# An attention over adjacency lists: when the first q rows, the fifth overlapped list tile, the first gathers and the later lists take their places

## The chip, the core and the metric

The kernel runs on one core of a Trainium2 chip. The time is the device time in microseconds, the median of several runs. A profile of one more execution shows what each engine did: PE (TensorE: matmuls; its weight loads are PEld), DVE (VectorE), ACT (ScalarE), POOL (GpSimd) and SP (SyncE, which here only issues DMAs). Each engine works through its own stream of instructions in order; ACT and POOL also issue DMAs from their streams.

## The reference

One layer of a graph network on N = 4096 nodes with D = 512 features and 8 heads of 64. `adj` is a 4096 x 4096 mask, symmetric, with ones on its diagonal and about 17 ones in a row.

```python
hs, ht = layer_norm(x), layer_norm(h_target)         # ln1, both masked by nodemask
q = (ht @ Wq + bq).reshape(T, 8, 64) / 8
k = (hs @ Wk + bk).reshape(S, 8, 64)
v = (hs @ Wv + bv).reshape(S, 8, 64)
logits = where(adj != 0, q . k, -1e30)               # per head
attn = softmax(logits) @ v @ Wo + bo
ht = layer_norm(ht + attn)                           # ln2
out = layernorm(x + ht + gelu(ht @ W1) @ W2)
```

Since a row of `adj` has so few ones, the kernel computes the attention on lists of neighbours and not on the full matrix. A flag is raised when the lists don't hold for the input; then a general path over the full matrix would run. It does not run here.

## The kernel before

**Lists.** Rows of `adj` come in 32 tiles of 128, each tile in 4 quarters of 1024 columns (512 KB); the quarters are numbered q = 4 x tile + h. `quarter` (L708) issues a quarter's load on SP (L713). `edges` (L716) works on it: ACT turns it to bytes and counts (L728, Sign), DVE multiplies by positions (L733) and takes the 8 largest in each of 5 segments (L735); after the fourth quarter DVE decodes the candidates into a record of up to 24 neighbours (L742 to L759), and the undecoded rest is written out later (`keep_rest`, L766, on SP). Three byte buffers (`signs`) stand between ACT and DVE. `sort` (L807) ranks 16 tiles' rows by degree, and POOL scatters their records to memory in that order (L853), once for tiles 0 to 15 (part 0, NA = 16) and once for tiles 16 to 31 (part 1).

**One ring for everything.** `ring` (L566) is 20 slots of one k|v row (1024 floats) per partition. While the lists are made, slots 0 to 7 take adjacency quarters (DEEP = 8), slots 8 to 11 h_target rows and later the k|v rows on their way out, slots 12 to 16 rows of x (`xrows`, L578); slots 17 and 18 are the two `wide` buffers, slot 19 holds small tools. Quarters of the tiles below NA + FILL = 21 go through slots 0 to 7, later ones (q84 on) through the two `wide` buffers in turn (L709 to L712). In the attention the slots take gathered k|v rows, 17 of them in the first half and 20 in the second. `place` (L1025) fixes ahead of time which slots each slot group of up to S = 3 neighbours uses, round and round, from slot 0.

**Projections.** `project` (L864) goes through x in 16 groups of two row tiles. `source` (L919) computes k and v of one row tile: 4 matmul steps with Wk and 4 with Wv (L929; the profile shows 8 matmuls for each), ACT copies each half out of PSUM (L931), and one DMA on ACT's queue writes the row tile to `kvd` in memory (L935). Three PSUM buffers (`pq`) lie between PE and ACT.

**Fronts.** `front(i)` (L982) makes the q rows of sorted tile i: POOL gathers the h_target rows by record (L988), DVE writes the scales with a tie to what `latest` names (L994; the tie is a real operand, so the instruction can't come before that tile is written), ACT scales (L998), PE transposes (L1002), ACT applies ln1 (L1005), PE multiplies with Wq (L1011), DVE finishes (L1016). `first_fronts` (L1154) makes two of them ahead of the attention: both records are loaded (`prefetch`, L970, L979), and then both fronts are begun. `latest` is set by `source` from group 14 on (L932), to a column of k; once the attention runs it is set by each slot group.

**Attention.** For each slot group POOL gathers k|v rows by record (L966 through `issue`, L1058, up to 4 groups ahead, 5 in the second half), DVE multiplies k by q (L1220) and sums per head (L1225), ACT takes the exp (L1229, L1238) and scales one of three v rows (L1204), DVE scales the other two (L1184), and PE adds them up by transposing into PSUM (L1192). `finish` (L1077) normalises a tile (L1082 to L1103: DVE, ACT, PE in turn) and applies Wo (L1111, L1115) and ln2. `feed` (L1310) is the feed-forward network of a group of two tiles: PE L1325, gelu on ACT L1328, PE L1334, and `end` for the last layer norm.

**What sets the order.** Generators yield costs, and `_weave` (L400) always goes on with the stream that is least far; the scheduler below it then takes each engine's instructions in that order of priority, but lets a later one go first where an earlier one isn't ready by its own reckoning. What comes out is one fixed order per engine. Streams up to the attention: projections, `prepare` (lists 0 to 15, first sort, first fronts), `fill` (FILL = 5 more tiles of lists, 16 to 20). Streams from the attention on: attention, feed-forward, the other lists (`other_lists`, L1443, which begins at WAIT = 40 and takes 1.5 times each step's cost) followed by the second sort, and the loads of the last weights (L586, L587). UNIT = 60 is the cost of a group of two tiles.

Of the kernel before, what the change touches and what calls it, by code (L numbers as in the profile page):

```python
# [399 lines left out]
def _weave(*streams):  # L400

    live = [[t, n, g] for n, (g, t) in enumerate(streams)]
    asleep = []
    while live:
        s = min(live)
        cost = next(s[2], StopIteration)
        if cost is None:
            assert len(live) > 1  # L410
            asleep.append(s)
            live.remove(s)
            continue
        if cost is StopIteration:
            live.remove(s)
        else:
            s[0] += cost
        for w in asleep:
            w[0] = max(w[0], s[0])
        live += asleep  # L420
        asleep = []


def _take(gen, n):

    for _ in range(n):
        cost = next(gen, StopIteration)
        if cost is StopIteration:
            return
        yield cost  # L430
# [13 lines left out]
def adj_resnorm_kernel(  # L444
# [34 lines left out]
    N, D = x.shape  # L479
# [3 lines left out]
    NT = N // P  # L483
    G = 2
# [3 lines left out]
    NQ = 4  # L488
# [12 lines left out]
    NA, NBT = len(CAPS_A), len(CAPS_B)  # L501
# [31 lines left out]
    with tc.tile_pool(name="keep", bufs=1) as keep:  # L533
# [17 lines left out]
        with ExitStack() as late:  # L551
# [22 lines left out]
            def turn_of(name, places):  # L574
                turns[name] += 1
                return places[turns[name] % len(places)]
# [127 lines left out]
            adjs = []  # L704
            DEEP = 8
            FILL = 5

            def quarter(i, h):  # L708
                if i < NA + FILL:  # L709
                    a = ring[:, (i * NQ + h) % DEEP, :].bitcast(I32)  # L710
                else:
                    a = turn_of("wide", wide)  # L712
                nc.sync.dma_start(a, adj[i * P:(i + 1) * P, h * QW:(h + 1) * QW])  # L713
                return a

            def edges(i):  # L716

                part = 1 if i >= NA else 0
                rec = Rs[part][:, i - PARTS[part][0], :]
                cand = lp.tile([P, SEG, 8], U16, name="cand", bufs=2)  # L720
                for h in range(NQ):
                    n = i * NQ + h
                    while len(adjs) < min(n + 2, NT * NQ):
                        adjs.append(quarter(*divmod(len(adjs), NQ)))
                    a, adjs[n] = adjs[n], None

                    sg = turn_of("signs", signs)
                    nc.scalar.activation(sg, a, AF.Sign, accum_out=dpart[:, i, h:h + 1])  # L728
                    ahead = min(n + DEEP - 1, n + 3 + n // 2)
                    while len(adjs) < min(max(n + 3, min(ahead, (NA + FILL) * NQ)), NT * NQ):  # L730
                        adjs.append(quarter(*divmod(len(adjs), NQ)))
                    wd = sg.bitcast(U16)
                    nc.vector.tensor_tensor(wd, wd, lio, ALU.mult)  # L733
                    for s, (w0, w1) in enumerate(SEGS):
                        nc.vector.max(cand[:, h * SQ + s, :], wd[:, w0:w1])  # L735
                    if h == 1:
                        keep_rest()
                    if h % 2 and moms:
                        moments(moms.pop(0))
                    yield 2.0  # L740
                dec = dec_w
                nc.vector.tensor_single_scalar(dec[:, 0], cand, 255, op=ALU.bitwise_and)  # L742
                nc.vector.tensor_single_scalar(dec[:, 1], cand, 8, op=ALU.logical_shift_right)
                gid = lp.tile([P, 2 * SEG, 8], F32, name="gid")
                dec = dec.rearrange("p b s e -> p (b s) e")
                off = segoff.rearrange("p b q s -> p (b q s)")
                nc.vector.scalar_tensor_tensor(gid, dec, 0.0,
                                               off.unsqueeze(2).to_broadcast([P, 2 * SEG, 8]),
                                               op0=ALU.is_gt, op1=ALU.mult)
                nc.vector.tensor_add(gid, gid, dec)  # L750
                flat = gid.rearrange("p s e -> p (s e)")
                for r in range(RE // 8):
                    top = rec[:, E0 + r * 8:E0 + (r + 1) * 8]
                    nc.vector.max(top, flat)
                    if r + 1 < RE // 8:
                        nc.vector.match_replace(flat, top, flat, 0.0)
                held.append((rest_d[i * P:(i + 1) * P, :], flat))
                has = lp.tile([P, MAXE], F32, name="ehas")
                nc.vector.tensor_scalar(has[:, :RE], rec[:, E0:E0 + RE], 0.0, 0.0, op0=ALU.is_gt,  # L759
                                        op1=ALU.add, accum_out=cnt[:, i:i + 1])  # L760
                yield 4.0

            def keep_rest():

                while held:
                    nc.sync.dma_start(*held.pop())  # L766
# [33 lines left out]
            def moments(i):  # L800

                while asked and len(asked) > NT - 4 - i:
                    ask(asked.pop(0))
                t = hrow(i)
                stats(ip, t, mvh[:, i, :], "n0")
# [58 lines left out]
            def project(order, t=None):  # L864
# [54 lines left out]
                def source(n, j):  # L919
                    g, hT = order[n], state[n][1]  # L920
                    if asked or moms:
                        kvr = sp.tile([P, 2 * D], F32, name="tq", bufs=3)
                    else:

                        kvr = ring[:, 8 + (n * G + j) % 3, :]
                    for half, w in enumerate((wk, wv)):
                        pkv = psi.tile([P, D], F32, name="pq", bufs=3)
                        for kc in range(KC):
                            nc.tensor.matmul(pkv, hT[:, kc, j * P:(j + 1) * P], w[:, kc, :],  # L929
                                             start=kc == 0, stop=kc == KC - 1)  # L930
                        nc.scalar.copy(kvr[:, half * D:(half + 1) * D], pkv)  # L931
                    if n >= 14:  # L932
                        latest[:] = [kvr[:, 0:1]]
                    r0 = 1 + (g * G + j) * P
                    newest[:] = [nc.scalar.dma_start(kvd[r0:r0 + P, :], kvr).ins]  # L935
                    return 7.8
# [13 lines left out]
                for n in range(len(order)):  # L950
                    for j in range(G):
                        cost = source(n, j)
# [10 lines left out]
            recs, tqs, h2Ts, done, ready, latest, newest = {}, {}, {}, set(), [], [], []  # L963
# [6 lines left out]
            def prefetch(i):  # L970
                if i >= NT or i in recs:
                    return
                r0 = TILES[i][0]
                part = 1 if r0 >= PARTS[1][0] * P else 0
                assert part in done
                r0 -= PARTS[part][0] * P
                rec = sp.tile([P, E0 + MAXE], I32, name="rec", bufs=6)

                nc.gpsimd.dma_start(rec[:, :RW], recs_d[part][r0:r0 + P, :])  # L979
                recs[i] = rec  # L980
# [39 lines left out]
            EARLY = 2  # L1020
# [1 line left out]
            SG = [(i, j0, min(S, cap - j0)) for i, (_, cap) in enumerate(TILES)  # L1022
                  for j0 in range(0, cap, S)]
            kvs, rests, fronts = {}, {}, {}
            place = [0]  # L1025
            for i, _, n in SG:
                if place[-1] + n > RING[i >= NA]:
                    place[-1] = 0
# [6 lines left out]
            def step(gens, i):  # L1035

                if i in gens and next(gens[i], StopIteration) is StopIteration:
                    del gens[i]
# [111 lines left out]
            def go_on():  # L1150
                for i in list(fronts):
                    step(fronts, i)

            def first_fronts():  # L1154

                for i in range(EARLY):
                    prefetch(i)
                for i in range(EARLY):
                    fronts[i] = front(i)
                    step(fronts, i)  # L1160
                while not latest:
                    yield None
                while fronts:
                    go_on()
                    yield 4.0
# [210 lines left out]
            def chain(gens):  # L1376
                for g in gens:
                    yield from g

            WAIT = 40.0  # L1380
            AHEAD = 4
            UNIT = 60.0

# [36 lines left out]
            def fill():  # L1420
# [3 lines left out]
                yield 9.0  # L1424
                for cost in _take(ed, FILL * steps):
                    yield cost
# [16 lines left out]

            def other_lists():
                for cost in ed:
                    yield 1.5 * cost
                keep_rest()
                yield from sort(1)

            _weave((att, 0), (chain(feed(g) for g in range(len(GROUPS))), 0), (other_lists(), WAIT),  # L1450
                   (weights(), 0))

# [34 lines left out]
```

## Time and profile before

| | us |
|---|---|
| median of 3 runs (1814.98 to 1824.70) | 1821.21 |
| the profiled execution's own time | 1811.19 |
| its span | 1809.4 |
| busy in the span: PE / DVE / ACT / POOL | 1681.5 / 1435.1 / 1221.1 / 979.8 |
| PE busy from 290 to 350, of 60 us | 18.65 |
| median from issue to landing: an adjacency quarter / a k|v gather / a kvd write from the ring | 7.1 / 5.9 / 5.2 |

The profile's part 2 cuts the span in 40 slices of 45.2 us and shows for each the busy tenths of every engine, the granted clock of PE and the share and rate of the DMA engines. A line of the timeline has the start, the length, the engine, the line of the code, the operation with its output and input, how often, and in brackets how long the engine sat idle before it and what ended that. Tiles are named by the pool's tile: `kv` is the whole ring, so an adjacency quarter and a gathered k|v row both appear as `kv`. PE's clock is in shares of full speed, PE's ends are modelled, and the releaser in the brackets is inferred. An engine's queue of DMA issues has a q at its end (SPq, ACTq).

### The profile page before, as it was taken

The numbers are of one execution on the slowest core, as the hardware profiler recorded it, in microseconds if no ns is written. First come the engines' busy times: TensorE is split into PE (matmuls) and PEld (weight loads), VectorE is DVE, ScalarE is ACT, GpSimd is POOL, SyncE is SP. The second block draws the span as 40 slices with busy tenths as digits, with TensorE's granted clock in tenths as the row PEclk, the third lists the DMA queues.
The fourth block names the chain that finished last, engine by engine and source line by source line (L and its number), as shares of the span: only waits on it lengthen the run. The fifth ranks groups of instructions, "written<-read, shape, count | busy, mean of one in ns | idle before, by whom it ended". The sixth has DMA issues, their size and how long they took to land. (4 is left out here: it accounts for less than half of the span.)

```text
span 1809.4 us, 22969 instructions
## 1 busy us (share of the span) xinstructions
PE 1681.5 (93%) x7030; PEld 1101.4 (61%) x7030; DVE 1435.1 (79%) x2660; ACT 1221.1 (67%) x3119; POOL 979.8 (54%) x834
## 2 busy tenths in 40 slices
PE   7989984587999989999999989999999999999997
PEld 3434432465766666676776757666666666666664
DVE  6989886899999837777879989979879797988200
ACT  5767654486997636767768867877777676787211
POOL 1000144666566576667767788877575665663101
PEclk9999996698999999999999999999999999999998
DMA  9999968988887647778879888787776777774000
GB/s 343 370 376 375 344 228 293 405 276 321 294 300 237 230 159 258 240 253 279 281 256 320 288 263 292 252 281 261 242 273 216 255 239 247 247 246 149 18 6 26
DMA packets 140268, 463.26 MB, mean 256 GB/s; under 512 B 16500, under 2 KB 21672, under 8 KB 140136
## 3 DMA queue, kind: packets, MB, share of 16 engines
q0 software_dynamic: 96656, 342.64, 55.9%
q1 hardware_dynamic: 35664, 95.98, 15.0%
q10 hardware_dynamic: 7816, 23.08, 3.3%
q8 instruction: 58, 0.95, 0.2%
q14 instruction: 74, 0.61, 0.1%
HBM read 430.75 MB, written 30.89 MB: 255 GB/s over the span
## 5 line engine op out<-in xcount | busy, mean ns | idle before, releaser
L966 POOL DMA_INDIRECT kv<-kvd,rec x603 | 761.1, 1262 | 366.9 <-PE cps L1192 147.8
L1334 PE MATMUL po<-w,gt 128*128 128x512 f32 x1024 | 466.9, 598 | 10.3 <-ACT gt L1328 10.3
L1325 PE MATMUL pf<-h2T,w 128*128 128x256 f32 (+1 forms) x2176 | 466.5, 368 | 0.0
L1325 PEld LDWEIGHTS pf<-h2T,w 128*128 128x128 f32 x2176 | 389.7, 191 | 64.4 <-issue 19.8
L1220 DVE TENSOR_TENSOR kv<-kv,tq 128x1536 f32<-128x1536 f32 (+2 forms) x211 | 352.0, 1677 | 62.0 <-DMA kv<-kvd,rec 57.9
L1204 ACT ACTIVATE kv<-kv,pa 128x64 f32<-128x64 f32 x1520 | 390.9, 337 | 4.5
L1225 DVE TENSOR_REDUCE lg<-kv 128x24 f32<-128x1536 f32 (+2 forms) x211 | 350.4, 1668 | 1.2
L1334 PEld LDWEIGHTS po<-w,gt 128*128 128x128 f32 x1024 | 189.1, 192 | 207.2 <-issue 195.3
L1192 PE MATMUL cps<-ident,kv 128*128 128x128 f32 x2008 | 267.8, 282 | 47.7 <-DVE kv L1184 40.0
L1192 PEld LDWEIGHTS cps<-ident,kv 128*128 128x128 f32 x2008 | 242.2, 146 | 114.0 <-DVE kv L1184 45.8
L1184 DVE TENSOR_TENSOR kv<-kv,p 128x1024 f32<-128x1024 f32 (+1 forms) x211 | 251.3, 1195 | 23.8 <-ACT p L1229 22.5
L687 POOL TENSOR_TENSOR n_rs<-n_ve,mhalf 128x2 f32<-128x2 f32 (+2 forms) x51 | 48.6, 953 | 326.0 <-DVE n_ve L680 173.0
L728 ACT ACTIVATE kv<-kv 128x1024 uint8<-128x1024 int32 x128 | 134.9, 1055 | 94.5 <-DMA kv<-in_adj_dram 42.9
L1328 ACT ACTIVATE gt<-pf 128x512 f32<-128x512 f32 x128 | 76.3, 597 | 87.4 <-PE pf L1325 84.0
L1328 ACT ACT_TABLE_LOAD x103 | 132.1, 1283 | 1.7
L735 DVE MAX8 cand<-kv 128x8 uint16<-128x103 uint16 (+1 forms) x640 | 132.4, 253 | 0.5
L929 PE MATMUL pq<-wk,h2T 128*128 128x512 f32 x256 | 121.3, 619 | 8.3 <-ACT tq L931 5.7
L1229 ACT ACTIVATE p<-lg 128x24 f32<-128x24 f32 (+2 forms) x179 | 39.1, 218 | 120.5 <-DVE lg L1225 119.7
L1011 PE MATMUL t<-wq,tq 128*128 128x512 f32 x256 | 115.7, 595 | 2.1 <-ACT tq L1005 2.1
L929 PE MATMUL pq<-wv,h2T 128*128 128x512 f32 x256 | 115.4, 593 | 1.8 <-DVE rbc L662 1.0
L1115 PE MATMUL t<-wo,rb 128*128 128x512 f32 x256 | 115.2, 592 | 0.0
L929 PEld LDWEIGHTS pq<-wk,h2T 128*128 128x128 f32 x256 | 49.4, 199 | 65.3 <-issue 50.5
(160 smaller groups left out, 1581.8 us busy)
## 6 DMA issues: line engine op xcount, KB each, us to landing
kv<-in_adj_dram SPq DMA_DIRECT2D x128, 512.0 KB, 7.1
kvd<-tq ACTq DMA_DIRECT2D x24, 512.0 KB, 6.6
kv<-kvd,rec POOLq DMA_INDIRECT x603, 5.9
kv<-in_L_gnn_h_target_dram SPq DMA_DIRECT2D x32, 256.0 KB, 8.0
kv<-in_x_dram SPq DMA_DIRECT2D x15, 512.0 KB, 9.3
rest_d<-gid SPq DMA_DIRECT2D x32, 160.0 KB, 4.7
w<-in_L_gnn_W_dram SPq DMA_DIRECT2D x4, 1024.0 KB, 9.9
kvd<-kv ACTq DMA_DIRECT2D x8, 512.0 KB, 5.2
```

What stands on the lines that cost most here:

```text
L728: nc.scalar.activation(sg, a, AF.Sign, accum_out=dpart[:, i, h:h + 1])
L735: nc.vector.max(cand[:, h * SQ + s, :], wd[:, w0:w1])
L929: nc.tensor.matmul(pkv, hT[:, kc, j * P:(j + 1) * P], w[:, kc, :], start=kc == 0, stop=kc == KC - 1)
L966: nc.gpsimd.indirect_dma_start(out=dst, out_offset=None, in_=table[:, :], in_offset=bass.IndirectOffsetOnAxis(ap=idx, axis=0))
L1184: nc.vector.tensor_tensor(v4, v4, p[:, j0:j0 + m, :].unsqueeze(3) .to_broadcast([P, m, H, HD]), ALU.mult)
L1192: nc.tensor.matmul(cps[:, c, :], kv[:, j, D + c * P:D + (c + 1) * P], ident, is_transpose=True, start=j0 + j == 0 and c == 0, stop=j0 + n ...
L1204: newest[:] = [nc.scalar.mul(v, v, pa[:, hd:hd + 1]).ins]
L1220: nc.vector.tensor_tensor(kv[:, :n, :D], kv[:, :n, :D], tq[:, :D].unsqueeze(1).to_broadcast([P, n, D]), ALU.mult)
L1225: nc.vector.tensor_reduce(lg[:, :n, :], kv[:, :n, :D].rearrange("p j (h d) -> p j h d", h=H), AX.X, ALU.add)
L1325: nc.tensor.matmul(pf[:, k, :], w1[(f0 + k) // KC][:, kc, (f0 + k) % KC * P:((f0 + k) % KC + 1) * P], h2T[:, kc, :w], start=kc == 0, stop= ...
L1328: nc.scalar.activation(gt, pf, AF.Gelu_apprx_tanh)
L1334: nc.tensor.matmul(po[j], gt[:, k, j * P:(j + 1) * P], w2[(f0 + k) // KC][:, (f0 + k) % KC, :], start=False, stop=f0 + k == FC - 1, skip_g ...
```

## The change

Five edits. The tie of the first fronts names the last written half (v) of the last row tile instead of any k half from group 14 on. `first_fronts` loads a record and begins its front, tile by tile, instead of loading both records first. Tiles 0 to 19 use the ring's slots for their quarters (RINGED = 20), tile 20 uses the `wide` buffers. Slot groups are placed from slot 11 on. The other lists begin at 80 instead of 40 in the weave's cost and take 1.8 times each step's cost instead of 1.5. No engine gets other operations; the orders differ.

```diff
--- before.py
+++ after.py
@@ -704,9 +704,10 @@
             adjs = []
             DEEP = 8
             FILL = 5
+            RINGED = NA + FILL - 1
 
             def quarter(i, h):
-                if i < NA + FILL:
+                if i < RINGED:
                     a = ring[:, (i * NQ + h) % DEEP, :].bitcast(I32)
                 else:
                     a = turn_of("wide", wide)
@@ -727,7 +728,7 @@
                     sg = turn_of("signs", signs)
                     nc.scalar.activation(sg, a, AF.Sign, accum_out=dpart[:, i, h:h + 1])
                     ahead = min(n + DEEP - 1, n + 3 + n // 2)
-                    while len(adjs) < min(max(n + 3, min(ahead, (NA + FILL) * NQ)), NT * NQ):
+                    while len(adjs) < min(max(n + 3, min(ahead, RINGED * NQ)), NT * NQ):
                         adjs.append(quarter(*divmod(len(adjs), NQ)))
                     wd = sg.bitcast(U16)
                     nc.vector.tensor_tensor(wd, wd, lio, ALU.mult)
@@ -929,8 +930,8 @@
                             nc.tensor.matmul(pkv, hT[:, kc, j * P:(j + 1) * P], w[:, kc, :],
                                              start=kc == 0, stop=kc == KC - 1)
                         nc.scalar.copy(kvr[:, half * D:(half + 1) * D], pkv)
-                    if n >= 14:
-                        latest[:] = [kvr[:, 0:1]]
+                    if n * G + j == NT - 1:
+                        latest[:] = [kvr[:, D:D + 1]]
                     r0 = 1 + (g * G + j) * P
                     newest[:] = [nc.scalar.dma_start(kvd[r0:r0 + P, :], kvr).ins]
                     return 7.8
@@ -1022,7 +1023,7 @@
             SG = [(i, j0, min(S, cap - j0)) for i, (_, cap) in enumerate(TILES)
                   for j0 in range(0, cap, S)]
             kvs, rests, fronts = {}, {}, {}
-            place = [0]
+            place = [11]
             for i, _, n in SG:
                 if place[-1] + n > RING[i >= NA]:
                     place[-1] = 0
@@ -1155,7 +1156,6 @@
 
                 for i in range(EARLY):
                     prefetch(i)
-                for i in range(EARLY):
                     fronts[i] = front(i)
                     step(fronts, i)
                 while not latest:
@@ -1377,7 +1377,7 @@
                 for g in gens:
                     yield from g
 
-            WAIT = 40.0
+            WAIT = 80.0
             AHEAD = 4
             UNIT = 60.0
 
@@ -1443,7 +1443,7 @@
 
             def other_lists():
                 for cost in ed:
-                    yield 1.5 * cost
+                    yield 1.8 * cost
                 keep_rest()
                 yield from sort(1)
 
```

The new numbers of lines are one higher between `RINGED` and `first_fronts`, and the same after it.

## The prediction

> **What bounds the kernel now.** I read the page's parts 1 and 2 first, then a table of windows, then the timeline of the valley that part 2 shows, then ACT's waits.
>
> ```profile
> span 1809.4 us, 22969 instructions
> PE 1681.5 (93%) x7030; PEld 1101.4 (61%) x7030; DVE 1435.1 (79%) x2660; ACT 1221.1 (67%) x3119; POOL 979.8 (54%) x834
> PE   7989984587999989999999989999999999999997
> PEclk9999996698999999999999999999999999999998
> ```
>
> PE is busy to the end, while DVE, ACT and POOL run out some 100 us earlier. PE's instructions stay the same, so the time can only change by PE's idle time (1809.4 - 1681.5 = 127.9 us) and by the clock. Slices 6 and 7 (271 to 362 us) are the valley: there the projections end and the attention begins. The windows, in the order PE, PEld, DVE, ACT, POOL, clock, DMA share, GB/s:
>
> ```profile
> 290.00:310.00 20.00, 2.75 (x7) 0.95 (x5) 13.07 (x46) 5.75 (x10) 10.14 (x11) 0.67 0.90 316
> 310.00:330.00 20.00, 9.14 (x36) 7.06 (x36) 15.89 (x17) 8.49 (x33) 13.22 (x11) 0.50 1.03 407
> ...
> 430.00:450.00 20.00, 12.36 (x55) 10.40 (x56) 20.00 (x39) 14.88 (x47) 12.77 (x12) 0.66 0.89 338
> 450.00:500.00 50.00, 50.00 (x227) 35.20 (x226) 46.13 (x109) 45.63 (x110) 27.64 (x23) 1.00 0.85 288
> ```
>
> From 290 to 370 PE idles 17.3 + 10.9 + 13.2 + 4.4 = 45.8 us, from 410 to 450 another 1.5 + 7.6 = 9.1; from 450 on it is full, DVE or no DVE. The valley's timeline says why (start, length):
>
> ```profile
> 273.06 0.81 ACT L998 ACTIVATE tq<-tq,rec 128x512 f32<-128x512 f32 x1 [9.30 <-DVE gid L750]
> ...
> 282.38 1.06 ACT L728 ACTIVATE kv<-kv 128x1024 uint8<-128x1024 int32 x1 [4.05 <-DMA kv<-in_adj_dram]
> ...
> 290.03 0.33 ACTq L935 DMA_DIRECT2D kvd<-kv  x1
> ...
> 296.81 0.96 POOL L966 DMA_INDIRECT kv<-kvd,rec  x1 [20.42 <-ACT kv L728]
> ...
> 308.02 1.77 DVE L1220 TENSOR_TENSOR kv<-kv,tq 128x1536 f32<-128x1536 f32 x1 [1.98 <-DMA kv<-kvd,rec]
> ...
> 314.89 2.82 PE L1192 MATMUL cps<-ident,kv 128*128 128x128 f32 x12 [22.14 <-DVE kv L1184]
> ```
>
> L998, the scaling of the first q rows, holds ACT for 9.3 us while copies of k|v wait behind it. The last write of kvd goes out at 290.03; writes of kvd land after 4.3 to 6.0 us there, so at about 296; the first gather starts at 296.81. Its wait is put down to ACT's L728, but its slots 0 to 2 held adjacency quarters (q = 4 x tile + h) 80 to 82, which ACT read at 245.5 to 248.7. I take the landing of the last kvd write for the true releaser. ACT's waits from 220 to 460:
>
> ```profile
> ACT kv L728 <- DMA kv<-in_adj_dram: 22.3, 7, 4.1
> ```
>
> Those seven waits are of the tiles behind the ring (q84 on), which have two buffers only. They stand in ACT's order among the last copies of k|v.
>
> **What the Trainium skill says.** (1) "TensorE: Matmul & The Clock Gate", Architectural detail: ACT and DVE are strict FIFOs. The trace agrees: behind the 9.30 us of L998 no copy of k|v starts. (2) The same page, What's actually happening: after about 3.4 us without work the array runs at half clock. The clock of 0.50 at 310 to 330 agrees. (3) "DMA: Bandwidth & Descriptors", Anatomy of one DMA: about 2.0 us plus bytes/436e3; for a quarter of 512 KB that is an estimate of 3.2 us. The trace has 6.3 us from issue to landing at 245 to 262, 4.6 at 260 to 296 and 7.2 at 294 to 316; the measurements decide. (4) The same page, Issuing engines are not separate DMA queues: SP's loads and POOL's gathers share the DMA engines; 4.6 growing to 7.2 as the gathers begin agrees.
>
> **The change part by part**, against the profiled execution (1811.2 us with 1809.4 of span; the runs' median is 1821.2, 0.55% above it).
>
> *The tie moves to the last k|v copy, and the two fronts interleave.* In the built order PE's 8 transposes L1002 and ACT's two L998 go behind the last source's 16 matmuls and two copies instead of ahead of them; the h_target gathers stay first on POOL. Gone: ACT's 9.3 us and PE's 7.9 us wait at L1002. By itself that could bring the last kvd write from 290.0 to about 281. New: DVE's tie L994 now waits for the last copy, with the rest of tile 22's list decode behind it on DVE (six operations of about 0.5 us, which nobody awaits then), and both q rows begin only there. Their cost after the last copy: L994 0.4, L998 0.8, transposes 1.1, L1005 1.5, L1011 at half clock up to 5, L1016 0.7 = 9.5 us. The gathers need 6 (landing) + 0.8 + 11.2 (296.81 to 308.02) = 18 us: hidden, with 8 us to spare. Were that cover gone, it would cost those microseconds one for one.
>
> *Fifth fill tile outside the ring.* q80 to q83 no longer come through 8 slots but through the two wide buffers, as q84 on do. In the order 13 quarters, q80 to q92, stand ahead of the last copy of v. A buffer's cycle is the landing, 1.06 of L728 and about 0.6 of semaphores, SP and ACT; two buffers turn, so a quarter takes half. SP issues q81 at 242.3, when the sort frees the buffer (as q85 now: 242.27); landed at 248. With 6.3 us up to 262 and 4.6 after: q83 255.5, q85 263, q87 269.1, q89 275, q91 280.7; q82 252.7, q84 260.2, q86 266, q88 271.8, q90 277.6, q92 283.5. q92 read at 284.6, v's copy at 285.3, last kvd write **285.4**. The step moves four more quarters to the slow path and gives back about half of the 9 us. Net of both edits: 290.0 - 285.4 = **-4.6 us**; with 7.2 us landings it is +9.9, without any chain it is -9.
>
> *First gathers to slots 11 to 16 (place 11).* If the kvd landing is the releaser, 0: x's last row was read before 262. If the page's releaser (L728 at 296.4) is right, it adds nothing beyond the kvd landing either, since that follows 290.03 + 6. Bounds -0.5 to 0. The same sequence shifted modulo 17 afterwards: 0.
>
> *Lists later and further apart (80 for 40, 1.8 for 1.5).* These are due times; the built order says what they become. Ahead of the first exp ACT has q93 to q96 instead of q93 to q98: L1238 at 313.38 stood behind q98 (312.32) for **-1.5 us**. Until the eighteenth multiply (L1220) both orders have nearly no list work. Then DVE takes q97 to q103 between its 18th and 20th multiply (before: q99 to q105 between the 17th and 20th): the same seven, so the 9.1 us of PE's idle time at 410 to 450 stay. ACT has one quarter more ahead of the fourth tile's L1238: one L728 of **+1.1 us**, and up to 3.7 if its load is late. Between the 20th and 29th multiply lists fall from eight quarters (q106 to q113) to one, which is 7 x 2.3 = 16 us of DVE (a quarter: 0.41 + 0.93, and 3.9 per tile for decoding); PE is full from 450 on, so it earns 0, bound -3. They return in bursts, q105 to q114 at the 29th and 30th: 10 x 2.3 = 23 us of DVE, seven quarters of it on ACT with at most 4.4 us each. PE's own order has two hidden and three output steps, 36 transposes and a wo step there, some 29 us of work: hidden, bound +8. If that cover is gone PE waits for an L1192.
>
> *Second half's scatters (L853) later.* They fall to tiles 11 and 12 instead of 9; rec's load for tile 16 now stands directly behind the last scatter. POOL then waits 3.0 us, as at 266, with about 14 slots of gathers ahead: 0, bounds 0 to +3. SP's rest_d writes move only among its own loads: 0.
>
> Sum: -4.6 - 1.5 + 1.1 = **-5.0 us**: 1811.2 - 5.0 = 1806.2, a ratio of 0.9972; on the median 1821.2 it is **1816.2 us**.
>
> **The rivals.** *Faster.* The valley shortens as forecast, and the list work that leaves DVE takes the idle time of 410 to 450 along. For it: DVE is at 20.00 of 20 there, and three L728 wait between 417.8 and 427.5 ahead of L1238. Against it: the order puts seven quarters into the same hole. -6.1 - 9.1 - 2 of half clock = -17: 1794 x 1.0055 = 1804 us. *Slower: the two wide buffers become the bound.* One mechanism: every quarter from q80 on turns at half of (landing + 1.7). At 7.2 us that is 4.4 us; q92 is read at 249.5 + 11 x 4.4 = 298, the last kvd write leaves at 299.9 (+9.9), the burst at L1238 costs +3 and seven quarters at 4.4 outrun PE's 29 us by +4.5; less 1.5 of q98: +16, 1827 x 1.0055 = 1837 us. It decides from a landing of about 5.6 us on, where q92 comes at 288. For it: 7.1 us is the page's median; against it: 4.6 in this very stretch. *The slot edits do nothing* is part of the forecast.
>
> **How the numbers follow.** About 0.5% (9 us) is what a measurement can tell from no change. Forecast 0.40, faster rival 0.34, slower rival 0.26; they are the chances of same, faster and slower. Predicted 1816; its own range by the bounds above (-9.5 to +4 us) is 1811 to 1825. For 8 in 10 it reaches to both rivals: 1801 to 1836.
>
> **What would show it.** Right: ACT's wait of 9.3 us at L998 is gone; the last L935 starts at 281 to 289; the first L966 into kv follows it by 6 to 7 us, whatever slot it takes; the first L1220 lies at 303 to 305; PE idles as before at 410 to 450. Wrong: a last L935 after 290 with more than 22.3 us of waits of L728 for DMA (the slower rival); PE full from 400 on (the faster); a first L1220 that waits for L1016 and not for a gather (the cover of 8 us was not there); PE waits for L1192 or L1098 about 500 to 600.

## The result and the profile after

The changed kernel takes **1866.36 us** (median of 4 runs, 1861.8 to 1867.5) against 1819.74 for the kernel before: a ratio of **1.0258, interval 1.0236 to 1.0280**. The forecast was 1816 with a range up to 1836; the time lies 30 us above it. The kernel became slower, as the slower rival had it, and by more than that rival gave.

The page of the changed kernel (span and instructions, busy times, PE and its clock in 40 slices):

```profile
span 1859.9 us, 22946 instructions
PE 1688.8 (91%) x7030; PEld 1101.9 (59%) x7030; DVE 1438.5 (77%) x2660; ACT 1210.3 (65%) x3111; POOL 980.8 (53%) x834
PE   7989984596979799998999998999999999999997
PEclk9999996798989899999999998999999999999999
```

The span is 50.5 us longer. PE's busy time grew by 7.3 us with the same 7030 matmuls, and its idle time from 127.9 to 171.1, by 43.2. The slices say where (counted from 0, as in the prediction): the valley in 6 and 7 looks as it did, but slice 9 is deeper (6 for 7), and slices 11, 13 and 18 (7, 7 and 8) are new holes in a stretch that was full. In windows of 100 us, first before, then after (PE, PEld, DVE, ACT, POOL, clock, DMA share, GB/s):

```profile
400.00:500.00 100.00, 90.83 (x430) 64.63 (x429) 95.08 (x220) 79.58 (x205) 60.30 (x49) 0.93 0.87 301
500.00:600.00 100.00, 98.15 (x433) 66.11 (x432) 96.07 (x204) 77.94 (x190) 63.09 (x51) 1.00 0.81 276
600.00:700.00 100.00, 92.97 (x414) 63.20 (x413) 62.34 (x72) 59.16 (x164) 67.01 (x61) 0.97 0.59 199
...
800.00:900.00 100.00, 98.55 (x470) 69.73 (x469) 85.51 (x85) 73.58 (x206) 71.03 (x61) 1.00 0.80 276
```

```profile
400.00:500.00 100.00, 85.66 (x408) 60.35 (x407) 90.04 (x187) 76.16 (x201) 54.59 (x47) 0.93 0.79 277
500.00:600.00 100.00, 88.31 (x377) 59.62 (x376) 82.04 (x176) 65.96 (x168) 52.78 (x43) 0.93 0.74 256
600.00:700.00 100.00, 84.38 (x365) 56.93 (x365) 71.50 (x135) 60.09 (x156) 47.36 (x40) 0.91 0.58 195
...
800.00:900.00 100.00, 87.44 (x400) 59.84 (x399) 63.20 (x73) 57.98 (x150) 73.19 (x67) 0.97 0.70 234
```

From 400 to 700 PE idles 41.7 us instead of 18.1, from 800 to 1000 another 17.8 instead of 4.5, from 1000 to 1300 16.7 instead of 11.6. Up to 400 the two differ by 1.3 us only. Each table is of one execution, and executions differ: the kernel hl_before below, which loses nothing (0.9998), has 21.3, 8.3 and 13.4 us of idle time in these three stretches (its profile is of the slowest of its 20 executions). So the first two differences stand out clearly, and the third hardly. Over 400 to 700 as a whole DVE, ACT and POOL are all less busy than before. I read that not as one engine that became the bound, but as engines that wait for each other in turn.

The valley itself, by the timeline of the changed kernel (its lines are one higher than before in this part of the code):

```profile
291.26 0.33 ACTq L936 DMA_DIRECT2D kvd<-kv  x1
...
298.30 0.94 POOL L967 DMA_INDIRECT kv<-kvd,rec  x1 [4.04 <-DMA rest_d<-gid]
...
309.35 1.76 DVE L1220 TENSOR_TENSOR kv<-kv,tq 128x1536 f32<-128x1536 f32 x1 [6.46 <-DMA kv<-kvd,rec]
...
313.40 0.22 ACT L1238 ACTIVATE p<-lg 128x24 f32<-128x24 f32 x1 [6.60 <-DVE lg L1225]
...
314.94 2.82 PE L1192 MATMUL cps<-ident,kv 128*128 128x128 f32 x12 [10.64 <-DVE kv L1184]
```

The last kvd write goes out at 291.26 (before 290.03), the first exp at 313.40 (before 313.38), the first transposes of values at 314.94 (314.89). The edits at the front, which most of the prediction's working was about, moved these times by 1.2 us at most when taken together.

One hole from close by, on ACT and PE of the changed kernel (start, length; in brackets the idle time before and what ended it):

```profile
427.48 1.47 PE L1192 MATMUL cps<-ident,kv 128*128 128x128 f32 x12
429.63 1.06 ACT L729 ACTIVATE kv<-kv 128x1024 uint8<-128x1024 int32 x1 [5.20 <-DMA kv<-in_adj_dram]
...
436.06 1.06 ACT L729 ACTIVATE kv<-kv 128x1024 uint8<-128x1024 int32 x1 [3.53 <-DMA kv<-in_adj_dram]
...
437.11 0.21 ACT L1238 ACTIVATE p<-lg 128x24 f32<-128x24 f32 x1
...
438.40 0.62 ACT L1093 COPY rb<-ri 128x512 f32<-128x512 f32 x1
...
439.07 1.11 PE L1099 MATMUL t<-ident,rb 128*128 128x128 f32 x4 [10.12 <-ACT rb L1093]
```

PE waits 10.12 us for a 0.62 us copy (L1093). What it copies was ready on DVE at 418.24 (L1090), 20 us earlier. But the copy stands on ACT behind list quarters (L729), and those wait 5.20 and 3.53 us for their adjacency loads. Between 419.27 and 436.06 ACT does five quarters, one every 4.2 us. That is the pace of two buffers that turn: the loads of the kernel before land after 6.6 us (median from 400 to 560), and with 1.7 us around it half a cycle is 4.15. The prediction had this pace (4.4) in its slower rival, with too small a price.

A later hole is of the same kind. ACT's L1006 makes the rows that PE's L1012 multiplies, and it stands behind a quarter that waits for its load:

```profile
607.70 1.06 ACT L729 ACTIVATE kv<-kv 128x1024 uint8<-128x1024 int32 x1 [2.99 <-DMA kv<-in_adj_dram]
...
610.65 1.50 ACT L1006 ACTIVATE tq<-t,b1r,cols 128x128 f32<-128x128 f32 x4
...
611.15 6.36 PE L1012 MATMUL t<-wq,tq 128*128 128x512 f32 x8 [6.42 <-ACT tq L1006]
```

Not every hole is. At 654 PE waits 9.20 us for an ACT instruction too, but no quarter stands before that one: ACT waits for DVE's sums (5.73 us), and DVE had waited for a k|v gather (4.50 us). Loads of ACT's function tables are not the loss either: the trace has 198 of them, where the kernel before has 206.

### The profile page after: what moved, and what is told of

Same layout as the page of the kernel before. It is cut to its first block, busy times and chain, and to the rows that moved or that the text cites. A ratio compares the mean times of both kernels' runs of the same rounds, so it can differ in the third digit from the quotient of the medians.

```text
span 1859.9 us, 22946 instructions
## 1 busy us (share of the span) xinstructions
PE 1688.8 (91%) x7030; PEld 1101.9 (59%) x7030; DVE 1438.5 (77%) x2660; ACT 1210.3 (65%) x3111; POOL 980.8 (53%) x834
## 5 line engine op out<-in xcount | busy, mean ns | idle before, releaser
L967 POOL DMA_INDIRECT kv<-kvd,rec x603 | 750.5, 1245 | 362.2 <-PE cps L1192 164.5
L1220 DVE TENSOR_TENSOR kv<-kv,tq 128x1536 f32<-128x1536 f32 (+2 forms) x211 | 351.6, 1676 | 92.1 <-DMA kv<-kvd,rec 76.5
L1192 PE MATMUL cps<-ident,kv 128*128 128x128 f32 x2008 | 267.0, 282 | 58.3 <-DVE kv L1184 47.7
L1192 PEld LDWEIGHTS cps<-ident,kv 128*128 128x128 f32 x2008 | 241.4, 146 | 126.1 <-DVE kv L1184 54.8
L729 ACT ACTIVATE kv<-kv 128x1024 uint8<-128x1024 int32 x128 | 135.0, 1057 | 131.9 <-DMA kv<-in_adj_dram 75.5
L930 PE MATMUL pq<-wk,h2T 128*128 128x512 f32 x256 | 120.8, 617 | 12.4 <-ACT tq L932 7.8
L1012 PE MATMUL t<-wq,tq 128*128 128x512 f32 x256 | 120.6, 615 | 11.4 <-ACT tq L1006 10.8
L930 PE MATMUL pq<-wv,h2T 128*128 128x512 f32 x256 | 117.2, 601 | 7.4 <-ACT kv L932 6.2
L930 PEld LDWEIGHTS pq<-wv,h2T 128*128 128x128 f32 x256 | 48.9, 192 | 71.1 <-issue 59.0
```

What stands on the lines that cost most here:

```text
L967: nc.gpsimd.indirect_dma_start(out=dst, out_offset=None, in_=table[:, :], in_offset=bass.IndirectOffsetOnAxis(ap=idx, axis=0))
L1192: nc.tensor.matmul(cps[:, c, :], kv[:, j, D + c * P:D + (c + 1) * P], ident, is_transpose=True, start=j0 + j == 0 and c == 0, stop=j0 + n ...
L1220: nc.vector.tensor_tensor(kv[:, :n, :D], kv[:, :n, :D], tq[:, :D].unsqueeze(1).to_broadcast([P, n, D]), ALU.mult)
```

## The experiments

Eighteen kernels; each ratio is to the kernel before on the same chip, with its interval. "Built order" is the order in which instructions stand on an engine. The code shows only the lines that matter.

**Which edits cost.** The five edits in two halves: the front (tie with interleaved fronts, tile 20 outside the ring, place 11) and the list times; then the two list times apart.

```diff
 front3:  tie, RINGED = NA + FILL - 1, place = [11];  WAIT = 40.0, 1.5 * cost as before
 lists:   WAIT = 80.0, yield 1.8 * cost;              nothing else
 wait:    WAIT = 80.0 alone
 apart:   yield 1.8 * cost alone
```

> Before with the tie, the fifth list tile outside the ring and place 11, but with the list times of before (40, 1.5). Theory (the bunching of the list work is the cost; the front of the attention moves nothing): ratio 0.997 to 1.003; last kvd write near 291, first exp near 313 as in both traces, ACT waits less than 10 us for adjacency quarters between 400 and 700. Rival 1 (the two wide buffers under tile 20 are the cost): ratio 1.015 to 1.027.

> Before with the two list times alone (80, 1.8). Theory: ratio 1.018 to 1.028, and ACT waits 25 to 45 us for adjacency quarters between 400 and 700, in bunches of five or more, as in the changed kernel. Rival 1 (the fifth list tile): 0.997 to 1.003. Rival 2 (it takes both, since the bunches grow only with one more tile on two buffers): 1.005 to 1.012.

> Before with the later start alone (80, with 1.5). In the built order the quarters stand in bunches of 6, 10, 6 and 4, as with both. Theory (bunches): 1.012 to 1.025. Rival 3 (the cost is that the lists end later, by their spacing): under 1.006, and the spacing alone carries it.

> Before with the wider spacing alone (1.8, with 40). In the built order the quarters stand in bunches of 6, 5, 3 and 5 with single ones between. Theory (bunches): between before and the later start alone, 1.005 to 1.015. Rival 3 (spacing is the cost): 1.018 to 1.028.

Measured: front3 **1.0024** (1.0008 to 1.0040), lists **1.0296** (1.0265 to 1.0326), wait 1.0217 (1.0181 to 1.0253), apart 1.0193 (1.0144 to 1.0241). The list times are the whole loss; alone they cost at least as much as all five edits. Either one of them brings most of it. Rival 3 held that the spacing carries the cost and that the later start stays under 1.006; the later start cost 2.2%, so it falls. But the spacing alone came out in that rival's range (1.018 to 1.028), above what the theory had given it (1.005 to 1.015).

Why does work that is *due* later and further apart come in bunches? The due times decide only in which order the program is written. In the built order of DVE, list quarters stand between the attention's multiplies (L1220) like this; 97 quarters lie ahead of the first multiply and 2 behind the fifth in each of the rows:

```text
kernel    quarters behind multiply number ...                                                     ratio
before    17:1 18:1 19:5 22:1 23:1 24:1 25:2 26:1 27:1 28:1 29:2 30:1 32:1 33:2 35:2 36:3 39:1 40:2   1
apart     19:6 24:1 25:1 26:1 28:2 29:1 30:5 35:1 36:3 40:2 41:1 42:5                             1.0193
wait      19:6 26:1 28:4 30:6 35:1 36:6 41:1 42:4                                                 1.0217
lists     19:6 27:1 28:4 30:6 35:1 36:3 40:2 42:6                                                 1.0296
```

With the old times most quarters stand singly, one or two to a multiply. With the later ones they stand in bunches, mostly of four to six and with ten at 28 and 30 together, at the same few places (19, 28 to 30, 35 or 36, 42) and well ahead of their due points. That this comes from the builder is my reading, and no run shows it: a quarter whose turn comes late is moved up only where the builder expects its engine to have nothing else ready. The expected gaps are few, so the quarters gather in them.

**Is it the bunches?** The same list times, but each L728 from q99 on is tied behind ACT's last multiply by slot that was written before it, so that it can't be moved ahead of its due point (`held_back` is set where `other_lists` begins). As a control, the same tie with the old times.

```diff
+                    if held_back and n >= 99:
+                        with tc.issue_after(newest[-1]):
+                            nc.scalar.activation(sg, a, AF.Sign, accum_out=dpart[:, i, h:h + 1])
+                    else:
                         nc.scalar.activation(sg, a, AF.Sign, accum_out=dpart[:, i, h:h + 1])
 hl_lists:  WAIT = 80.0, 1.8 * cost      hl_before:  WAIT = 40.0, 1.5 * cost
```

> Before with both list times (80, 1.8), and every L728 from q99 on tied behind the last of ACT's by-slot multiplies issued so far, so that list work cannot be placed ahead of its own due point. In the built order at most four quarters stand between two multiplies (six with the list times alone), and the last comes at multiply 59. Theory (the bunches are the cost, not the lateness): 0.997 to 1.008, ACT waits under 12 us for adjacency quarters between 400 and 700. Rival (later list work costs by being later: second half sorted later, DVE loaded later): 1.018 to 1.03.

> Before with its own list times (40, 1.5), and every L728 from q99 on tied behind ACT's work at its due point: at most four quarters between two multiplies, the scatters where they were. Theory: 0.998 to 1.004, so that what the held lists with late times cost beyond it (1.0159) is lateness. Rival (tying costs by itself): 1.008 to 1.016.

Measured: hl_lists **1.0159** (1.0133 to 1.0186), hl_before **0.9998** (0.9985 to 1.0012). Tying costs nothing that can be measured. Without bunches the late times still cost 1.6%: the theory was half right, and so was the rival. The two costs are not parts of one sum, though. With the list times alone the bunches are early: ACT's last quarter starts at 610 us (561 before). With the quarters held it starts at 707. So holding them trades bunches for lateness, and what the bunches cost by themselves is at least the difference of 1.4%, if lateness is no gain; no run gives it alone. The windows of the kernel with the list times alone, and of the one with the quarters held:

```profile
400.00:500.00 100.00, 89.45 (x426) 62.72 (x425) 90.06 (x203) 77.13 (x199) 56.77 (x50) 0.95 0.82 288
500.00:600.00 100.00, 88.07 (x374) 59.08 (x373) 82.34 (x168) 66.33 (x167) 49.84 (x39) 0.90 0.73 245
600.00:700.00 100.00, 85.69 (x371) 57.86 (x369) 70.42 (x120) 59.95 (x157) 44.85 (x43) 0.93 0.60 199
...
800.00:900.00 100.00, 89.61 (x395) 61.94 (x394) 68.57 (x77) 57.52 (x157) 74.31 (x65) 0.93 0.72 241
```

```profile
400.00:500.00 100.00, 95.44 (x448) 67.16 (x447) 80.58 (x138) 68.22 (x182) 58.64 (x52) 0.95 0.76 258
500.00:600.00 100.00, 92.20 (x402) 62.20 (x401) 83.71 (x161) 70.78 (x180) 48.02 (x46) 0.97 0.73 256
600.00:700.00 100.00, 97.92 (x451) 68.25 (x450) 88.28 (x177) 77.17 (x193) 57.83 (x51) 1.00 0.82 281
...
800.00:900.00 100.00, 82.56 (x372) 57.13 (x371) 74.17 (x83) 67.68 (x192) 70.96 (x63) 0.93 0.76 256
```

PE's idle time from 400 to 700 is 36.8 us with the bunches and 14.4 without (before 18.1): there the whole loss goes with the bunches. From 800 on holding the quarters doesn't bring the idle time back: 800 to 1000 has 18.5 and 20.9 us (before 4.5). ACT's waits for adjacency loads, from 400 to 1000, with the list times alone and with the quarters held:

```profile
ACT kv L728 <- DMA kv<-in_adj_dram: 38.8, 14, 6.9
```

```profile
ACT kv L730 <- DMA kv<-in_adj_dram: 2.9, 2, 2.7
```

**Are the bunches dear by ACT's waits, or by their own work?** Here the loads of the last seven list tiles are left out (their lists are made of what the two buffers still hold), and with them the flag's test and the slow path. The list work on ACT and DVE stays, and so do the bunches in the built order.

```diff
-                nc.sync.dma_start(a, adj[i * P:(i + 1) * P, h * QW:(h + 1) * QW])
+                if i < 25:
+                    nc.sync.dma_start(a, adj[i * P:(i + 1) * P, h * QW:(h + 1) * QW])
...
-    left = nc.values_load(flag[0:1, 0:1], min_val=0, max_val=1)
-    with tc.If(left != 0):
-        general_path(...)
 nl_before:  WAIT = 40.0, 1.5 * cost      nl_lists:  WAIT = 80.0, 1.8 * cost
```

> Before with the adjacency loads of the last seven list tiles (q100 on) left out, so that their lists are made of what the buffers still hold, and with the test of the flag and the slow path behind it left out. The list work on ACT and DVE is as before, 28 loads of 512 KB are gone. Both theories: 0.990 to 1.0 (it is the base for the next run).

> The same with both list times (80, 1.8): bunches of 6, 7 and 5 quarters as in the changed kernel, but no L728 from q100 on has a load to wait for. Theory (ACT's waits for the two buffers are what the bunches cost): 1.005 to 1.015 above the run without loads and with the old times, which is the lateness. Rival (the list work itself in one place is the cost, loads or not): 1.022 to 1.03 above it.

Measured: nl_before 0.9943 (0.9923 to 0.9964), nl_lists 1.0153 (1.0129 to 1.0178). The second is 1.0153 / 0.9943 = **1.0211** of the first. With loads the same step was 1.0296, so about 0.8 of the 3% go with the loads. That may be ACT's waits for them or their traffic beside the gathers; this edit takes out both. The number falls between theory and rival, and nearer to the rival. PE's idle time from 400 to 700 rises from 12.2 to 26.8 us, by 14.6 without loads against 18.7 with them. So most of the loss stays where no load can be waited for. I read it as the list work standing in one place on DVE and ACT, ahead of products that PE waits for; the late scatters of the next runs are in it too, and no kernel without loads had its quarters held. In that kernel PE still waits 5.04, 5.80 and 5.87 us at the same three transposes (L1099, at 431, 530 and 633) for ACT.

**The late part: the scatters?** From 800 to 900 POOL's 16 scatters of the second half (L853) and two loads of rec had come to stand directly ahead of the tiles that need them. They alone are moved:

```diff
                 keep_rest()
+                yield 80.0
                 yield from sort(1)
 ls80: with everything else as before      hl_ls80: with the quarters held, old list times
```

> Before with 80 more of due time ahead of the second half's sort alone: the list quarters stay where they were, and in POOL's built order the 16 scatters L853 and the two rec loads behind them stand exactly as in the changed kernel (196 to 206 gathers in, before 144 to 149). Theory (the second part of the loss is the place of the scatters: 16 of 1.4 us each in POOL's way just ahead of the tiles that need them): 1.005 to 1.012, PE idle of 10 to 18 us between 800 and 1000. Rival (the prediction's step, hidden behind the gathers in flight): 0.998 to 1.003.

> Before with its own list times, every L728 from q99 on held at its due point, and the sort of the second half 80 later, so that the scatters stand where the changed kernel has them. Theory 1 (the lateness of the list quarters themselves is the open part): 1.001 to 1.005, the sum of the two edits alone. Theory 2 (late scatters and spread quarters make it together): 1.010 to 1.017.

Measured: ls80 **1.0021** (1.0008 to 1.0034), hl_ls80 1.0071 (1.0046 to 1.0097). PE with late scatters, then PE before:

```profile
819.80 5.29 PE L1334 MATMUL po<-w,gt 128*128 128x512 f32 x8 [15.46 <-ACT gt L1328]
```

```profile
667.49 6.15 PE L1334 MATMUL po<-w,gt 128*128 128x512 f32 x8 [5.43 <-ACT gt L1328]
...
819.01 3.70 PE L1334 MATMUL po<-w,gt 128*128 128x512 f32 x8 [1.45 <-ACT gt L1328]
```

The hole is there, 15.46 us in one piece as the theory had it (20.5 us of idle time from 800 to 1000). But the 5.43 us behind the earlier scatters, at 667, are gone. In all, the profile has 8.4 us more of idle time (136.3 for 127.9), and the ratio is worth 3.8 us (1.5 to 6): it lies in the rival's range. A wait that is seen in one place is not yet a loss in the sum. With held quarters the same move costs 0.7%, between the two theories.

> Before with the later start alone (80, with 1.5), every L728 from q99 on held at its due point. The last quarter comes at multiply 48 (42 with the old times, 59 with both), the scatters at 165 to 171 gathers (144 and 194). Theory 1 (cost grows with lateness): 1.004 to 1.010, between the two ends. Theory 2: under 1.004, since the scatters are not at their deadline.

With held quarters and part of the lateness (`WAIT = 80.0`, 1.5 as before) the ratio was **1.0097** (1.0064 to 1.0131). So lateness costs by degrees (0.9998, 1.0097, 1.0159), and not only where the scatters meet their deadline: theory 1. What in it costs the 0.9 to 1.4% beyond the scatters (1.0159 against 1.0071 with held quarters or 1.0021 without) is **open**. PE idles 18.6 us from 1000 to 1300 with held quarters and late times (11.6 before, 13.4 in hl_before), hundreds of microseconds after the last list quarter, and no run takes that apart.

**The front, edit by edit.**

```diff
 tie:       if n * G + j == NT - 1: latest[:] = [kvr[:, D:D + 1]], one loop for both fronts; nothing else
 ringed:    RINGED = NA + FILL - 1 alone
 tie_ring:  both
 tie_f6:    tie, FILL = 6 (one tile more through the ring)
 tie_f6p:   tie, FILL = 6, place = [11]
```

> Before with the tie at the last copy of v and the interleaved fronts alone. By the prediction's working the last kvd write moves from 290 to about 281: ratio 0.995. Rival (nothing of it is kept, since the copies wait for the two wide buffers and for PE as before): 0.998 to 1.003, last kvd write after 286.

> Before with the fifth list tile outside the ring alone. By the prediction's working four more quarters at about 3 us each, behind L998's wait as well: ratio 1.002 to 1.006, last kvd write 293 to 298. Rival (hidden in the 9 us of L998): 0.998 to 1.002.

> Before with the tie and the fifth list tile outside the ring, place 0. The three front edits together gave 1.0024, the tie 0.9968, the tile 1.0012. Theory (place 11 does nothing; with the tie the four quarters are no longer hidden in L998's wait): 1.001 to 1.004, last kvd write near 289. Rival (place 11 costs): 0.996 to 0.999.

> The same with place 0. Theory (the landing of the last kvd write lets the first gathers go, whatever slot they take): within 0.002 of the run with place 11. Rival (slots 0 to 2, which now hold quarters for longer, hold them back): 0.002 to 0.006 above it.

> Before with the tie, place 11, and one more list tile (six for five) ahead of the attention through the eight ring slots, so one less on the two wide buffers: the other way from the change. Theory: the waits of L728 for the wide buffers among the last copies (17.9 us with the tie alone) shrink to about 10, the last kvd write comes at 277 to 283, scatters at 131 to 133: 0.990 to 0.997. Rival (the ring slots are then read later than the first gathers want them): 0.998 to 1.004.

```text
kernel     last kvd write  first gather  first L1220  first exp   ratio (interval)
before         290.03         296.81        308.02      313.38
tie            282.74         289.05        297.81      302.27    0.9968 (0.9952 to 0.9984)
ringed         290.73         297.77        308.36      312.08    1.0012 (1.0000 to 1.0024)
tie_ring       290.57         297.74        308.98      313.04    0.9990 (0.9976 to 1.0004)
front3         289.21         295.16        306.66      310.71    1.0024 (1.0008 to 1.0040)
tie_f6         288.16         295.61        307.68      311.74    0.9989 (0.9976 to 1.0002)
tie_f6p        287.51         294.54        304.03      308.08    1.0032 (1.0018 to 1.0046)
```

Of the kernels that do all the work the tie alone has the lowest ratio, and its interval lies below 1; the gain is smaller than the 0.995 worked out for it. Its valley:

```profile
282.74 0.33 ACTq L935 DMA_DIRECT2D kvd<-kv  x1
...
289.05 0.94 POOL L966 DMA_INDIRECT kv<-kvd,rec  x1 [3.50 <-DMA kvd<-kv]
...
297.81 1.76 DVE L1219 TENSOR_TENSOR kv<-kv,tq 128x1536 f32<-128x1536 f32 x1 [1.56 <-DMA kv<-kvd,rec]
...
302.27 0.21 ACT L1237 ACTIVATE p<-lg 128x24 f32<-128x24 f32 x1
```

Tile 20 outside the ring takes the earlier start back (290.57 for 282.74; the intervals of the two ratios overlap). From 230 to the last kvd write ACT waits 18.9 us for adjacency loads, 14.0 with the tie alone, and PE waits 3.4 us for a copy of k|v (L930 for L932), 0.7 with the tie alone. In tie_ring ACT in turn waits for PE, with a quarter that has landed behind it:

```profile
265.84 0.59 ACT L932 COPY kv<-pq 128x512 f32<-128x512 f32 x1 [3.21 <-PE pq L930]
266.32 1.06 ACT L729 ACTIVATE kv<-kv 128x1024 uint8<-128x1024 int32 x1
```

Without the tie (ringed) tile 20 stayed in its rival's range, hidden or nearly so. One tile *more* through the ring does not help either: tie_f6p came out in its rival's range. And place 11 costs 0.3 to 0.4% in both pairs (tie_ring to front3, tie_f6 to tie_f6p), although the first exp comes 2.3 and 3.7 us earlier with it. The rival of tie_ring had said so; tie_f6 fits neither of its two texts, which had place 11 level or ahead. Why it costs is **open**; no one place in the traces shows the loss.

**Lists the other way.** Two last runs ask whether earlier or closer lists gain.

```diff
 held_before: the tie of every L728 from q84 on (not q99), WAIT = 40.0, 1.5 * cost
 tie_c140:    tie, yield 1.4 * cost
```

> Before with its own list times (40, 1.5), and every L728 from q84 on tied behind ACT's work at its due point. The built order has 84 quarters ahead of the first multiply for 97. Theory: no quarter of the two wide buffers stands before the last copies of k and v, so the last kvd write goes out at 275 to 284 and the ratio is 0.985 to 0.998. Rival (the same quarters then load DVE and ACT between multiplies 7 and 17, where PE starves): 1.0 to 1.012.

> Before with the tie and the list spacing 1.4 in place of 1.5: the lists the other way, a little closer together, so that no bunch is over four quarters. Theory: 0.990 to 0.998, not behind the tie alone (0.9968). Rival (each microsecond of list work in the valley costs): 0.998 to 1.005.

Measured: held_before **1.0092** (1.0065 to 1.0119), tie_c140 1.0065 (1.0041 to 1.0090). In the first, 13 quarters fewer stand before the first multiply. The last kvd write goes out at 284.32 and the first exp at 300.13, 13 us before that of the kernel before, and the kernel is slower all the same; the rival was right. Windows of the kernel before, then of this one:

```profile
300.00:340.00 40.00, 11.48 (x44) 8.71 (x44) 30.79 (x47) 13.95 (x48) 27.55 (x24) 0.50 1.02 395
340.00:400.00 60.00, 49.66 (x271) 38.25 (x272) 56.62 (x76) 43.64 (x130) 40.95 (x33) 0.85 0.90 328
```

```profile
300.00:340.00 40.00, 18.61 (x81) 14.74 (x82) 31.54 (x39) 18.47 (x67) 28.41 (x25) 0.55 1.01 392
340.00:400.00 60.00, 39.29 (x230) 29.24 (x229) 54.10 (x129) 39.50 (x100) 30.70 (x24) 0.89 0.85 307
400.00:500.00 100.00, 85.31 (x382) 60.05 (x381) 97.21 (x225) 78.04 (x206) 58.96 (x46) 0.90 0.83 294
```

The 7 us won up to 340 are lost with 10 from 340 to 400 and 5.5 more up to 500, where the quarters now stand between the first multiplies. In the second run quarters a little closer together cost 1% against the tie alone, although no bunch was to be over four: the theory that closer lists are safe fell, and the result lies above the rival's range as well. PE idles 14.2 us from 1200 to 1300 there (2.35 with the tie alone), again long after the lists (hl_before has 6.5 there). Of the list times that were run the old ones are the best, and a kernel can lose against them without bunches.

## Why the prediction was wrong, step by step

- **The tie.** Right. Alone it was to bring the last kvd write from 290.0 to about 281; it came at 282.74, and the ratio was 0.9968, where 0.995 was worked out. Of the 11.1 us by which the first exp moved, some 5 arrive in the time. PE starts earlier, but idles 29.6 us from 300 to 340 (before 28.5), while the DMA engines are full (share 1.03).
- **Tile 20 outside the ring.** The mechanism was right and the size off: "gives back about half of the 9 us". It gave back all of it (290.57 with both edits, 285.4 was worked out). The term at fault is the chain of 13 quarters. By its own terms (landing + 1.06 + 0.6) a buffer's cycle is 6.3 us at the end, where it counts about 5.8, so q92 lands at 285.7 and not at 283.5. And it left out that PE, held by copies of k|v behind late quarters, makes the next copies late in turn: the 3.21 us at 265.84 shown above. The 3.2 us for a quarter, worked out from the Trainium skill ("DMA: Bandwidth & Descriptors", Anatomy of one DMA), was no estimate for these loads: that section is about DMAs that GpSimd issues, and SP issues the quarters. They took 4.6 to 7.2 us, and the 3.2 went into no sum.
- **The landing of the last kvd write lets the first gather go**, not L728. Right, as far as shown: the gather follows it by 6.0 to 7.5 us in every row of the table, whatever slot it takes, and with the tie alone the trace names the landing. With the adjacency loads moved out of the way (held_before) it follows after 3.57 us, and there too the trace names it. In the other rows the page names something else.
- **Place 11 at nothing.** Wrong by 6 to 8 us (0.34 and 0.43%), cause open.
- **Lists: "it earns 0, bound -3" and "hidden, bound +8".** This is the step that failed, in three ways. First the cover. It read the burst of q105 to q114 in the built order (at the 29th and 30th multiply) and set it against PE's own work queued at that place, 29 us. But PE's queue does not run by itself: its transposes, output steps and q projections wait for ACT's copies and activations, and those can stand behind the quarters in ACT's stream. That burst runs on ACT from 482 to 525, and from 500 to 600 PE idles 9.8 us more than before, a little beyond the bound. Second, its reading ends at q114. The 13 quarters after that stand in two more bursts (on ACT from 552 to 570 and from 603 to 616), which it did not price; from 600 to 700 PE idles 8.6 us more. Third, the late times cost beyond the bursts: 18.4 us more idle time from 800 to 1300 (13.4 of it up to 1000, where the late scatters fall), and still 1.6% with no bursts at all. The cause of that is in part open.
- **The idle time of 410 to 450 stays.** It grew: PE idles 5.2 us more from 400 to 500, with one wait of 10.12 us at 439. Seven quarters stand there in both orders, now behind the 18th and 19th multiply alone.
- **Scatters, "0, bounds 0 to +3".** Nearly right in the sum (1.0021, 4 us, alone), for a wrong reason. They weren't hidden: a hole of 15.46 us opened, and another closed. With held quarters they cost 0.7%, beyond the bound.
- **The slower rival** named the right resource for part of it: two buffers at 4.2 us a quarter. It put the price at the front (+9.9), where it came out as +1.2, and gave the seven quarters of the burst +4.5. Measured, the bunches cost at least 1.4%, and what goes with the loads is 0.8%, some 15 us. Its sum also has a slip: at a landing of 5.6 us its own pace puts q92 at 289.7, not 288.
- **The clock.** PE's busy time was taken as fixed, 1681.5. In the profile it is 7.3 us more. That need not be the change: profiles of hl_before (ratio 0.9998) and hl_ls80 (1.0071) have 1688.5 and 1677.2. What a hole does to single matmuls is plain: in the timeline shown above, 4 transposes at L1099 take 1.11 us after the wait of 10.12 (0.66 us in the kernel before, at 431, after 2.68). The Trainium skill says so ("TensorE: Matmul & The Clock Gate", What's actually happening: the array drops to half clock when it has been without work); the trace agrees, with a clock of 0.91 to 0.93 from 400 to 700 in the changed kernel (0.93 to 1.00 before).

The prediction's own test said what would show it wrong: PE waiting for L1192 or L1098 about 500 to 600. That is what the trace has (L1192 2.36 us at 530, L1099, which was L1098, 3.75 at 543), and at 439 and 654 longer waits than there.

## What to carry to other kernels

A burst of side work is not safely covered by the work queued on the bound engine, if that work gets its inputs from an engine whose queue the burst stands in. Before you call it hidden, follow the bound engine's next inputs one engine back, and read the order to the last of the moved work. And where due times are only wishes to a builder, read in the built order what became of them: moving work later can bunch it, and starting the main stage earlier (13 us here) gained nothing where the side work then fell into its first steps.

## What the runs showed of the hardware

Where the trace names the landing of the last kvd write (512 KB) as what lets the first gather go, the gather starts 6.31 us after the write's issue with the tie alone and 3.57 us after it in held_before, which issues no adjacency load in the 40 us before. In the 4 us behind the write the DMA engines are busy to 0.84 and 0.32. So the landing of the same write took nearly twice as long where other transfers filled the DMA engines; that they are the cause is likely, and not isolated.
